# Regrouping the clustering's products and moving the next image's keys, queries and first scores, with the first transfers on two queues

## The chip, the cores and the metric

One core of one Trainium2 chip runs the kernel. The metric is device time in microseconds of one launch, the median of three runs. Everything is fp32.

## What is computed

The input x is four images of 256 channels by 64x64 points (N = 4096). Each image goes through two layers:

```python
# layer 0: attention over the 4096 points
attn = softmax((wq x + bq)^T (wk x + bk))
x = gamma * (wv x + bv) attn^T + x
# layer 1: clustering, then a perceptron
y = x + ls1 * cluster(group_norm1(x))
y = y + ls2 * (w2 gelu(w1 group_norm2(y) + b1) + b2)
z = relu(bn(y * dw_w));  z = relu(bn(pw_w z))
```

`cluster` works per head (4 of 24 channels) and per quarter of the image (2x2 folds). It pools 4 centres, gives each point to its most similar centre, averages the points of each centre (this needs the *count* of points per centre), and sends each centre's mean back to its points, weighted by the similarity, through `proj_w`. The group norms are over all channels and points of an image, so group_norm2 needs every point of y before its first output.

## The kernel before

The program is written out in a fixed order; every engine takes its instructions in that order and waits on semaphores. For each of the four images (loop at L1557) it runs `weighting` (the attention's weighted sums, L582), `cluster` (L693) and `mlp` (L1155). TensorE is kept busy across the seams: the next image's projections are a list of small closures (`parts.projections`, L686), and `fill(n)` issues the next n of them wherever the image at hand would make TensorE wait. The list holds 32 halves of v (L307; two share a PSUM bank and one ScalarE copy), and at place 26 `k_half(0)` (L283, keys), `q_four(0)` (L328, queries of four blocks) and `k_half(1)`. For the last image the list holds a block of the third image's perceptron instead (`late_block`, L1039).

The steps that the change and the prediction touch:

- **Start** (L100 to L115). All first loads are issued by SP, in this order: `wqk_s`, `pv_s` (per-partition parameters), four pieces of `bqk_s` (biases of q and k), the first two of the four x tiles (two DMAs of 512 KB each), `wv_s`, `gbv`, the other x tiles, `pc_s`, and so on. `alone` (L531) then projects keys (`kp`, L291) and queries (`qp`, L333), sends the queries to the four row bands through GpSimd's DMA queue, and projects v (`vp`, L314).
- **Count** (L920). After the eight blocks of `fv` (L868), TensorE sums the pooled v (`agg`, L898). VectorE takes norms, the largest similarity and a one-hot (L828 to L834, tile `scr`), which the `cnt` matmuls (L923) wait for. In between stand `similar(1, lambda: fill(2))` and `fill(3)`: the two fills come to five closures.
- **Products back to the points** (`products`, L979; row `op`, L993). There are 16 matmuls with 32 rows each: two halves hb of the points, two halves c of the channels, four quarters q. Quarter q uses rows 32q to 32q+31 of the array, so different quarters can run side by side. For c = 0 they go to `ps_s` banks and VectorE adds them into y (L1005); for c = 1 they go to the `ps_a` banks a0 and a1 (by q % 2), ScalarE scales them (L1017) and GpSimd adds them (L1018). `seen(hb, c)` takes the statistics for group_norm2 on VectorE, four at a time (L977). Five calls of `products` make four unbroken groups on TensorE, with fills between (L1022 to L1035).
- **Second norm** (`group_norm`, L239). VectorE aggregates the statistics (L243), TensorE averages over the partitions (`gnm`, L245 and L246), VectorE takes differences (L249 to L253), TensorE averages again (`gnv`, L255), then come the root on ScalarE and the scale and bias on VectorE. One fill stands after `gnm`, one after `gnv`, then all that is left.
- **Perceptron.** `mlp` first has GpSimd form sums of weights (L1168 to L1173), then norms block 0 (L1187, L1250 to L1253), then runs units (block nb, j) with j from 0 to 3: `hp`, `hq`, `hr` (L1372) and `mo` (L1289). After some units the next image's scores for its first queries are formed (`score`, L352; row `sc`, L363): `at` (L1463) says after which unit. Their copies go to ScalarE; their maxima wait in the list `maxima`, from which `rest` takes one before and one after each unit with j > 1.

Of the kernel before, what the change touches and what calls it, by code (L numbers as in the profile page):

```python
# [8 lines left out]
F32 = mybir.dt.float32  # L9
# [4 lines left out]
P = 128  # L14
# [3 lines left out]
NB = 512  # L18
NBLK = N // NB
XT = 1024  # L20
D = 32
# [24 lines left out]
def attention_then_cluster_block(  # L46
# [37 lines left out]
        nc.sync.dma_start(out=d.rearrange("(a b) -> a b", b=D), in_=rows)  # L84
        nc.sync.dma_start(out=dst, in_=d.partition_broadcast(P))

    def load_x(b, t):
        xb = x[b].rearrange("(k p) h w -> p k (h w)", p=P)
        xt = spool.tile([P, KC, XT], F32, tag="s", name=f"x_{b}_{t}")
        for k in range(KC):  # L90
            nc.sync.dma_start(out=xt[:, k, :], in_=xb[:, k, t * XT : (t + 1) * XT])
        return xt

    def loaded(name, ap, shape):
        t = const.tile(shape, F32, name=name)
        nc.sync.dma_start(out=t, in_=ap)
        return t


    wqk_s = const.tile([P, KC, 2, D], F32, name="wqk_s")  # L100
    for k in range(KC):
        nc.sync.dma_start(out=wqk_s[:, k], in_=wqk[k * P : (k + 1) * P, :, :D])
    pv_s = loaded("pv_s", pv, [P, NPV])
    bqk_s = const.tile([P, 2], F32, name="bqk_s")
    for r in range(RG):
        nc.sync.dma_start(
            out=bqk_s[r * D : (r + 1) * D, :], in_=pv[:D, PV["bq"] : PV["bq"] + 2]
        )
    xs0 = [load_x(0, t) for t in range(2)]
    wv_s = loaded("wv_s", wv.rearrange("(k p) m -> p k m", p=P), [P, KC, C])  # L110
    gbv = const.tile([P, KC], F32, name="gbv")
    nc.sync.dma_start(out=gbv, in_=bv.rearrange("(k p) -> p k", p=P))
    xs0 += [load_x(0, t) for t in range(2, N // XT)]
    pc_s = loaded("pc_s", pc.rearrange("(k p) n -> p k n", p=P), [P, KC, len(PC)])
    h64 = loaded("h64", consts[:, K_H64:K_BD], [P, 64])  # L115

# [52 lines left out]
    def rsqrt(dst, src, eps, meanwhile=lambda: None):  # L169

        nc.vector.tensor_scalar(dst, src, eps, None, ALU.add)
        nc.scalar.activation(dst, dst, AF.Sqrt)
        meanwhile()
        nc.vector.reciprocal(dst, dst)
# [60 lines left out]
    def table(f):  # L235

        nc.scalar.activation(probe, probe, f)

    def group_norm(b, which, stats, fill, meanwhile=lambda: None):  # L239

        nm = f"{which}_{b}"
        mv = small.tile([P, 2], F32, tag="mv", name=f"mv_{nm}")
        nc.vector.bn_aggr(mv, stats.rearrange("p i s -> p (i s)"))  # L243
        ps1 = ps_a.tile([P, NB], F32, tag="a0", name=f"gnm_{nm}")
        nc.tensor.matmul(ps1[:, 0:1], left, mv[:, 0:1], start=True, stop=True)  # L245
        nc.tensor.matmul(ps1[:, 1:2], avg, mv[:, 0:1], start=True, stop=True)  # L246
        fill(1)
        dv = small.tile([P, 2], F32, tag="dv", name=f"dv_{nm}")
        nc.vector.tensor_copy(dv, ps1[:, 0:2])  # L249
        nc.vector.scalar_tensor_tensor(  # L250
            mv[:, 1:2], dv[:, 0:1], dv[:, 0:1], mv[:, 1:2], ALU.mult, ALU.add
        )
        nc.vector.tensor_scalar(dv[:, 1:2], dv[:, 1:2], -1.0, None, ALU.mult)  # L253
        ps2 = ps_a.tile([P, NB], F32, tag="a1", name=f"gnv_{nm}")
        nc.tensor.matmul(ps2[:, 0:1], avg, mv[:, 1:2], start=True, stop=True)  # L255
        rstd = small.tile([P, 1], F32, tag="rstd", name=f"rstd_{nm}")
        rsqrt(rstd, ps2[:, 0:1], GN_EPS, meanwhile)
        fill(3 if which == "gn1" else 1)
        if which == "gn2":
            table(AF.Gelu_apprx_tanh)  # L260
        ga = small.tile([P, KC], F32, tag="ga", name=f"ga_{nm}")
        gb = small.tile([P, KC], F32, tag="gb", name=f"gb_{nm}")
        nc.vector.tensor_scalar(ga, par(f"{which}_w"), rstd, None, ALU.mult)
        nc.vector.scalar_tensor_tensor(gb, ga, dv[:, 1:2], par(f"{which}_b"), ALU.mult, ALU.add)
        return ga, gb
# [9 lines left out]
    def attention(b, xs):  # L275
# [408 lines left out]
        parts.score, parts.fold, parts.q_block = score, fold, q_block  # L684
        parts.maximum, parts.first, parts.exps = maximum, first, exps
        parts.projections = [lambda i=i: v_half(i) for i in range(N // P)]  # L686
        parts.projections[26:26] = [lambda: k_half(0), lambda: q_four(0), lambda: k_half(1)]
        return parts


    h64_q = h64[:ED].rearrange("p (q h m) -> p q h m", q=4, h=HEADS)

    def cluster(b, ys, stats, cells, rest, fill, gelu):  # L693

        pool = small.tile([P, KC, 4, 4], F32, tag="pool", bufs=1, name=f"pool_{b}")

# [107 lines left out]
        def over_m(t):  # L804
            return t.unsqueeze(2).to_broadcast([P, 64, 4])

        def similar(f, meanwhile=lambda: None):

            sg = sgs[f]

            def between():
                table(AF.Gelu_apprx_tanh)
                meanwhile()

            rsqrt(prns[f], prns[f], L2_EPS, between)
            nc.vector.tensor_tensor(quad(sg), quad(sg), over_m(prns[f]), ALU.mult)
            nc.scalar.activation(sg, sg, AF.Tanh, scale=ab[:, 0:1], bias=ab[:, 1:2])
            if f == 0:
                gelu(0)
                table(AF.Sqrt)  # L820
# [85 lines left out]
        fill(2)  # L906
        summed(lambda j, q: pool_w[:, j], True)
        heads(NBLK - 1)
        similar(1, lambda: fill(2))
        gelu(1)  # L910
        fill(3)
        table(AF.Sqrt)
# [63 lines left out]
            for q in range(4):  # L976
                nc.vector.bn_stats(stats2[:, 4 * q + 2 * hb + c, :], pieces[hb, c, q])  # L977

        def products(hb, c, qs):  # L979
            if c == 0:  # L980
                two = [
                    ps_s.tile([P, 2, NB], F32, tag="s", name=f"op_{b}_{hb}_{c}_{f}")
                    for f in range(2)
                ]
                ops = {q: two[q // 2][:, q % 2, :] for q in qs}
            else:
                ops = {
                    q: ps_a.tile([P, NB], F32, tag=f"a{q % 2}", name=f"op_{b}_{hb}_{c}_{q}")
                    for q in qs
                }  # L990
            for q in qs:
                rows = slice(q * 32, (q + 1) * 32)
                nc.tensor.matmul(  # L993
                    ops[q],
                    g_s[rows, c * P : (c + 1) * P],
                    sim_t[rows, hb, :],
                    start=True,
                    stop=True,
                )
            for q in qs:  # L1000
                y = pieces[hb, c, q] = ys[2 * (q // 2) + hb][:, c, :].rearrange(
                    "p (h f w) -> p f h w", h=16, f=2
                )[:, q % 2]
                if c == 0:
                    nc.vector.scalar_tensor_tensor(  # L1005
                        y,
                        ops[q].rearrange("p (h w) -> p h w", h=16),
                        par("ls1", c),
                        y,
                        ALU.mult,  # L1010
                        ALU.add,
                    )
                else:
                    add = work.tile(
                        [P, NB], F32, tag=f"w{(4 * hb + q) % 3}", bufs=1, name=f"cl_{b}_{hb}_{q}"
                    )
                    nc.scalar.activation(add, ops[q], AF.Identity, scale=par("ls1", c))  # L1017
                    nc.gpsimd.tensor_tensor(  # L1018
                        y, add.rearrange("p (h w) -> p h w", h=16), y, ALU.add
                    )  # L1020

        products(0, 0, range(4))  # L1022
        products(0, 1, (0, 1))
        seen(0, 0)
        fill(2)
        products(0, 1, (2, 3))
        fill(2)
        products(1, 0, range(4))
        products(1, 1, (0, 1))
        fill(2)  # L1030
        products(1, 1, (2, 3))
        seen(0, 1)
        seen(1, 0)
        seen(1, 1)
        fill(5)  # L1035
        return stats2


# [113 lines left out]
        nc.gpsimd.tensor_tensor(s2, s1, a11, ALU.subtract)  # L1152
        return s1, s2, w7

    def mlp(b, ys, stats2, fill, nxt, blocks, turned):  # L1155


        W_A, W_CD, W_B, W_D = own_w["q"]
# [101 lines left out]

        for _ in norm(0, nc.vector):
            pass
        if nxt:
            nxt.q_block(0, nc.sync)

        def product(out, w, j, x):
            nc.tensor.matmul(out, w[:, j * P : (j + 1) * P], x, start=True, stop=True)
# [179 lines left out]

        hooks, drips, maxima = [], [], []  # L1450

        def hook():
            while hooks:
# [6 lines left out]
        acc, todo, slots = None, iter(()), (0,) * 4  # L1460
        own = ahead = iter(())

        at = {(u, 3): u for u in range(7)} | {(7, 2): 7}  # L1463
        if blocks < NBLK:
            at |= {(6, 1): 6, (6, 2): 7}
            del at[6, 3]
# [86 lines left out]
    with tc.manual_schedule():  # L1553
        here = attention(0, xs0)
        here.alone()
        late = None
        for b in range(B):  # L1557
            xs1, begun = [], []
            nxt = attention(b + 1, xs1) if b + 1 < B else None

            def ahead():
                if nxt and len(xs1) < N // XT:
                    xs1.append(load_x(b + 1, len(xs1)))
                elif late and not begun:
                    begun.append(begin())

            begin, todo, gelu = late or (None, list(nxt.projections) if nxt else [], lambda i: None)
            fill = filler(todo)
            stats, cells, rest = here.weighting(ahead, fill, (lambda: None) if b else derived)
            turned = turn_w2(b, not nxt)  # L1570
            stats2 = cluster(b, here.xs, stats, cells, rest, fill, gelu)

            late = mlp(b, here.xs, stats2, fill, nxt, NBLK - (b == B - 2), turned)
            here = nxt


# [74 lines left out]
```

## Time and profile before

| | us |
|---|---|
| median of 3 runs | 3362.1 (3361.42 to 3362.94) |
| the profiled execution | 3361.72 |
| its span, first to last instruction | 3359.9 |
| TensorE busy | 3308.0 (98%) |
| VectorE busy | 2225.8 (66%) |
| GpSimd busy | 1930.0 (57%) |
| ScalarE busy | 1683.6 (50%) |
| mean granted TensorE clock | 0.998 |

In the lines below, a line gives start and duration in us, engine, source line, operation, output and inputs with shape and type, and in brackets the idle time of that engine before it and what ended it. PE is TensorE, PEld its weight loads, DVE VectorE, ACT ScalarE, POOL GpSimd, SP the queue that issues most DMAs. An fp32 matmul of the program is two records. The granted clock is a share of full speed.

### The profile page before, as it was taken

The numbers are of one execution on the slowest core, as the hardware profiler recorded it, in microseconds if no ns is written. First come the engines' busy times: TensorE is split into PE (matmuls) and PEld (weight loads), VectorE is DVE, ScalarE is ACT, GpSimd is POOL, SyncE is SP. The second block draws the span as 40 slices with busy tenths as digits, with TensorE's granted clock in tenths as the row PEclk, the third lists the DMA queues.
The fourth block names the chain that finished last, engine by engine and source line by source line (L and its number), as shares of the span: only waits on it lengthen the run. The fifth ranks groups of instructions, "written<-read, shape, count | busy, mean of one in ns | idle before, by whom it ended". The sixth has DMA issues, their size and how long they took to land.

```text
span 3359.9 us, 34780 instructions
## 1 busy us (share of the span) xinstructions
PE 3308.0 (98%) x12322; PEld 1807.2 (54%) x12322; DVE 2225.8 (66%) x3546; ACT 1683.6 (50%) x2253; POOL 1930.0 (57%) x1366
## 2 busy tenths in 40 slices
PE   8999999999999999999999999999999999999999
PEld 4333444788533344578843344457873344346786
DVE  4767764677666766467766676646766766665675
ACT  5555553545555554354555555434555555544444
POOL 2655666366365676646635566554644676673664
PEclk9999999999999999999999999999999999999999
DMA  2000002000000000200000000020000000010000
GB/s 72 13 13 10 14 9 86 4 13 20 25 13 13 13 13 17 76 4 20 15 27 13 10 13 13 22 71 4 20 26 13 13 13 13 10 40 1 13 20 26
DMA packets 43102, 70.99 MB, mean 21 GB/s; under 512 B 9680, under 2 KB 18480, under 8 KB 42928
## 3 DMA queue, kind: packets, MB, share of 16 engines
q1 hardware_dynamic: 38064, 61.94, 5.5%
q10 hardware_dynamic: 4608, 6.30, 0.8%
q8 instruction: 97, 1.59, 0.2%
q14 instruction: 77, 0.63, 0.1%
q0 software_dynamic: 256, 0.52, 0.1%
HBM read 43.46 MB, written 16.89 MB: 18 GB/s over the span
## 4 chain that ended last, share of the span: by engine, by line
PE 94%; DVE 5%; ACT 1%; issue 0%; POOL 0%; DMA 0%; SPq 0%; ACTq 0%; POOLq 0%; DVEq 0%
PE av L477 53%; PE mo L1289 10%; PE sc L363 8%; PE hq L1372 5%; PE hp L1372 3%; PE hr L1372 3%; PE vp L314 2%; PE fv L868 2%; PE mo L1273 1%; PE hq_pw L1372 1%; PE pw L1226 1%; PE hr_pw L1372 1%; PE op L993 1%; PE hp_pw L1372 1%; PE qp L333 0%; PE kp L291 0%
## 5 line engine op out<-in xcount | busy, mean ns | idle before, releaser
L477 PE MATMUL av<-s,v 128*128 128x512 f32 x4096 | 1819.2, 598 | 0.6 <-ACT s L467 0.6
L472 POOL TENSOR_TENSOR acc<-acc,s 128x1024 f32<-128x1024 f32 x448 | 1057.2, 2360 | 539.0 <-ACT s L467 520.2
L477 PEld LDWEIGHTS av<-s,v 128*128 128x128 f32 x4096 | 759.0, 190 | 1044.8 <-issue 1034.8
L467 ACT ACTIVATE s<-s 128x1024 f32<-128x1024 f32 x512 | 540.2, 1057 | 592.0 <-DVE s L464 550.6
L464 DVE TENSOR_TENSOR s<-s,mb 128x1024 f32<-128x1024 f32 x512 | 595.7, 1205 | 18.2 <-ACT mb L448 16.3
L385 DVE TENSOR_TENSOR top<-sc,top 128x1024 f32<-128x1024 f32 x196 | 239.4, 1221 | 374.8 <-PE sc L363 374.7
L1327 ACT ACTIVATE hs<-hs,pv_s 128x256 f32<-128x256 f32 x496 | 232.2, 502 | 340.1 <-DVE hs L1363 340.1
L1289 PE MATMUL mo<-hs,w 128*128 128x256 f32 x1512 | 387.8, 382 | 0.0
L381 ACT COPY s<-sc 128x1024 f32<-128x1024 f32 x224 | 224.8, 1003 | 225.6 <-PE sc L363 225.6
L1289 PEld LDWEIGHTS mo<-hs,w 128*128 128x128 f32 x1512 | 282.0, 190 | 60.1 <-ACT hs L1327 19.8
L363 PE MATMUL sc<-q,k 32*128 32x512 f32 x2048 | 300.0, 640 | 0.4 <-ACT s L386 0.4
L388 DVE TENSOR_TENSOR top<-sc,top 128x1024 f32<-128x1024 f32 x196 | 240.0, 1225 | 72.4 <-ACT s L381 59.3
L386 ACT COPY s<-sc 128x1024 f32<-128x1024 f32 x224 | 227.0, 1013 | 66.4 <-DVE top L383 36.1
L1363 DVE TENSOR_TENSOR hs<-hq,hs 128x256 f32<-128x256 f32 x496 | 198.6, 421 | 75.5 <-PE hq L1372 65.3
L469 POOL TENSOR_TENSOR acc<-s 128x1024 f32<-128x1024 f32 x32 | 75.3, 2353 | 287.5 <-ACT s L467 260.8
L1296 POOL TENSOR_TENSOR hs<-hs 128x256 f32<-128x256 f32 x108 | 82.3, 762 | 194.1 <-ACT hs L1380 91.4
L363 PEld LDWEIGHTS sc<-q,k 32*128 32x128 f32 x2048 | 86.4, 182 | 183.2 <-issue 122.0
L1363 DVE TENSOR_TENSOR hs<-hp,hs 128x256 f32<-128x256 f32 x124 | 52.1, 420 | 142.5 <-ACT hs L1380 142.5
L1372 PE MATMUL hr<-xn,w 128*128 128x256 f32 x496 | 127.5, 379 | 0.5 <-DVE hs L1363 0.5
L314 PE MATMUL vp<-wv_s,x 128*128 128x256 f32 x512 | 123.4, 387 | 0.2 <-ACT v L322 0.2
L314 PEld LDWEIGHTS vp<-wv_s,x 128*128 128x128 f32 x512 | 93.5, 190 | 25.5 <-issue 10.5
L1372 PEld LDWEIGHTS hr<-xn,w 128*128 128x128 f32 x496 | 94.1, 190 | 19.1 <-issue 4.8
(261 smaller groups left out, 3508.2 us busy)
## 6 DMA issues: line engine op xcount, KB each, us to landing
x<-in_x SPq DMA_DIRECT2D x32, 512.0 KB, 6.9
out<-xn SPq DMA_DIRECT2D x62, 256.0 KB, 2.1
w<-in_w SPq DMA_DIRECT2D x8, 1024.0 KB, 10.9
mr<-row_mx SPq DMA_DIRECT2D x28, 256.0 KB, 3.1
rden<-row_rd SPq DMA_DIRECT2D x28, 256.0 KB, 3.2
q<-q ACTq DMA_DIRECT2D x96, 64.0 KB, 2.0
mix<-in_wfv SPq DMA_DIRECT2D x8, 192.0 KB, 8.5
q<-q SPq DMA_DIRECT2D x24, 64.0 KB, 2.0
```

Of the source, the lines that this page charges most:

```text
L314: nc.tensor.matmul(vps[0][:, i % 2, :], xs[i * P // XT][:, k, o : o + P], wv_s[:, k, :], start=(k == 0), stop=(k == KC - 1),)
L363: nc.tensor.matmul(halves[r // 2][:, r % 2, :], k_s[rows, g, :], q_s[rows, :], start=True, stop=True)
L385: nc.vector.tensor_tensor(top, halves[1], top, ALU.max)
L388: nc.vector.tensor_tensor(top, halves[0], top, ALU.max)
L464: nc.vector.tensor_tensor(sh, sh, mxs[nb].unsqueeze(1).to_broadcast([P, 2, NB]), ALU.subtract)
L467: nc.scalar.activation(sh, sh, AF.Exp)
L472: nc.gpsimd.tensor_tensor(acc, acc, s[:, 2 * h : 2 * h + 2], ALU.add)
L477: nc.tensor.matmul(av[c], own["v"][:, RG * g + quarter, c * P : (c + 1) * P], slots[u][:, quarter, :], start=(g == 0 and quarter == 0), st ...
L1289: return nc.tensor.matmul(bank[:, half * HB : (half + 1) * HB], a[:, j], t, start=start, stop=stop)
L1327: nc.scalar.activation(src, src, AF.Gelu_apprx_tanh, bias=pvc("b1", P, j + 4 * (i > 1)))
L1363: nc.vector.tensor_tensor(dst, ps, term, ALU.add)
L1372: nc.tensor.matmul(out, w, x, start=True, stop=True)
```

## The change

It has five parts, and no arithmetic changes.

1. The first two DMAs (tile x_0) go on SP at once. The weights of q and k, tile x_1 and the biases are issued by ScalarE's queue, in this order; `pv_s` is loaded after the last x tile.
2. `k_half(0)` and `q_four(0)` move from place 26 of the list to place 16. In `cluster`, the fill of two no longer stands inside `similar(1)` but behind it, so that the tanh comes first on ScalarE.
3. The 16 products come in three groups, of six, six and four. The last two of (1, 1) go to a pair of `ps_s` banks instead of a0 and a1.
4. At the end of `cluster` stand the first queries' transfers (`q_block(0)`, before at L1264), a fill of four, and `score(0)`, before after unit (0, 3) of the perceptron. Without a next image, a fill of six stands there.
5. `group_norm` for gn2 has a fill of two after `gnm`, before one.

```diff
-    def load_x(b, t):
+    def load_x(b, t, dma=nc.sync):
...
-            nc.sync.dma_start(out=xt[:, k, :], in_=xb[:, k, t * XT : (t + 1) * XT])
+            dma.dma_start(out=xt[:, k, :], in_=xb[:, k, t * XT : (t + 1) * XT])
...
+    xs0 = [load_x(0, 0)]
...
-        nc.sync.dma_start(out=wqk_s[:, k], in_=wqk[k * P : (k + 1) * P, :, :D])
-    pv_s = loaded("pv_s", pv, [P, NPV])
+        nc.scalar.dma_start(out=wqk_s[:, k], in_=wqk[k * P : (k + 1) * P, :, :D])
...
+    xs0.append(load_x(0, 1, nc.scalar))
     for r in range(RG):
-        nc.sync.dma_start(
+        nc.scalar.dma_start(
...
-    xs0 = [load_x(0, t) for t in range(2)]
...
     xs0 += [load_x(0, t) for t in range(2, N // XT)]
+    pv_s = loaded("pv_s", pv, [P, NPV])
...
-        fill(1)
+        fill(1 if which == "gn1" else 2)
...
-        parts.projections[26:26] = [lambda: k_half(0), lambda: q_four(0), lambda: k_half(1)]
+        parts.projections[26:26] = [lambda: k_half(1)]
+        parts.projections[16:16] = [lambda: k_half(0), lambda: q_four(0)]
...
-        similar(1, lambda: fill(2))
+        similar(1)
+        fill(2)
...
+        def pair(hb, c, q):
+            two = ps_s.tile([P, 2, NB], F32, tag="s", name=f"op_{b}_{hb}_{c}_{q}")
+            return [((hb, c, q + i), two[:, i, :]) for i in range(2)]
+
+        def single(hb, c, q):
+            return (hb, c, q), ps_a.tile(
+                [P, NB], F32, tag=f"a{q % 2}", name=f"op_{b}_{hb}_{c}_{q}"
+            )
+
-        products(0, 0, range(4))
-        products(0, 1, (0, 1))
+        products(*pair(0, 0, 0), *pair(0, 0, 2), single(0, 1, 0), single(0, 1, 1))
         seen(0, 0)
         fill(2)
-        products(0, 1, (2, 3))
+        products(single(0, 1, 2), single(0, 1, 3), *pair(1, 0, 0), *pair(1, 0, 2))
         fill(2)
-        products(1, 0, range(4))
-        products(1, 1, (0, 1))
-        fill(2)
-        products(1, 1, (2, 3))
+        products(single(1, 1, 0), single(1, 1, 1), *pair(1, 1, 2))
         seen(0, 1)
         seen(1, 0)
         seen(1, 1)
-        fill(5)
-        return stats2
+        if not nxt:
+            fill(6)
+            return stats2
+
+        nxt.q_block(0, nc.sync)
+        fill(4)
+        copies = []
+        nxt.score(0, copies, maxima)
+        copies.pop()()
+        return stats2
...
-        if nxt:
-            nxt.q_block(0, nc.sync)
...
-        at = {(u, 3): u for u in range(7)} | {(7, 2): 7}
+        at = {(u, 3): u for u in range(1, 7)} | {(7, 2): 7}
```

More of the change, by code (lines that the diff above doesn't have):

```diff
@@ L686, in attention, with cluster @@
         parts.projections = [lambda i=i: v_half(i) for i in range(N // P)]
-        parts.projections[26:26] = [lambda: k_half(0), lambda: q_four(0), lambda: k_half(1)]
+        parts.projections[26:26] = [lambda: k_half(1)]
+        parts.projections[16:16] = [lambda: k_half(0), lambda: q_four(0)]
         return parts
     h64_q = h64[:ED].rearrange("p (q h m) -> p q h m", q=4, h=HEADS)
-    def cluster(b, ys, stats, cells, rest, fill, gelu):
+    def cluster(b, ys, stats, cells, rest, fill, gelu, nxt, maxima):
         pool = small.tile([P, KC, 4, 4], F32, tag="pool", bufs=1, name=f"pool_{b}")
@@ L805, in over_m, with similar @@
             return t.unsqueeze(2).to_broadcast([P, 64, 4])
-        def similar(f, meanwhile=lambda: None):
+        def similar(f):
             sg = sgs[f]
[L811 to L815, printed above, removed]
+            rsqrt(prns[f], prns[f], L2_EPS, lambda: table(AF.Gelu_apprx_tanh))
             nc.vector.tensor_tensor(quad(sg), quad(sg), over_m(prns[f]), ALU.mult)
@@ L977, in seen, with products @@
                 nc.vector.bn_stats(stats2[:, 4 * q + 2 * hb + c, :], pieces[hb, c, q])
[L979 to L991, printed above, removed]
+        def products(*jobs):
+            for (hb, c, q), bank in jobs:
                 rows = slice(q * 32, (q + 1) * 32)
                 nc.tensor.matmul(
-                    ops[q],
+                    bank,
                     g_s[rows, c * P : (c + 1) * P],
@@ L999, in products @@
                 )
-            for q in qs:
+            for (hb, c, q), bank in jobs:
                 y = pieces[hb, c, q] = ys[2 * (q // 2) + hb][:, c, :].rearrange(
@@ L1006, in products @@
                         y,
-                        ops[q].rearrange("p (h w) -> p h w", h=16),
+                        bank.rearrange("p (h w) -> p h w", h=16),
                         par("ls1", c),
@@ L1016, in products @@
                     )
-                    nc.scalar.activation(add, ops[q], AF.Identity, scale=par("ls1", c))
+                    nc.scalar.activation(add, bank, AF.Identity, scale=par("ls1", c))
                     nc.gpsimd.tensor_tensor(
@@ L1153, in turn_w2, with mlp @@
         return s1, s2, w7
-    def mlp(b, ys, stats2, fill, nxt, blocks, turned):
+    def mlp(b, ys, stats2, fill, nxt, blocks, turned, maxima):
         W_A, W_CD, W_B, W_D = own_w["q"]
@@ L1446, in finish @@
             return lambda: relu(1)
-        hooks, drips, maxima = [], [], []
+        hooks, drips = [], []
         def hook():
@@ L1570, in attention_then_cluster_block @@
             turned = turn_w2(b, not nxt)
-            stats2 = cluster(b, here.xs, stats, cells, rest, fill, gelu)
-            late = mlp(b, here.xs, stats2, fill, nxt, NBLK - (b == B - 2), turned)
+            maxima = []
+            stats2 = cluster(b, here.xs, stats, cells, rest, fill, gelu, nxt, maxima)
+            late = mlp(b, here.xs, stats2, fill, nxt, NBLK - (b == B - 2), turned, maxima)
             here = nxt
```

## The prediction

> **What bounds the kernel now.** I read the page first, then who waited for whom on TensorE, then the order of time in the start and in one clustering.
>
> ```profile
> PE 3308.0 (98%) x12322; PEld 1807.2 (54%) x12322; DVE 2225.8 (66%) x3546; ACT 1683.6 (50%) x2253; POOL 1930.0 (57%) x1366
> ```
>
> TensorE is busy 98% of the span, and the change neither adds nor removes a matmul. So the time can only come from TensorE's waits, and from places where its rows lie side by side better. The waits of TensorE (us in total, times, longest):
>
> ```profile
> PE kp L291 <- DMA x<-in_x: 9.7, 3, 8.7
> PE cnt L923 <- DVE scr L834: 5.4, 4, 1.4
> PE hp L1372 <- DVE xn L1251: 3.9, 4, 1.5
> PE gnm_gn L245 <- DVE mv_gn L243: 3.8, 4, 3.2
> PE gnv_gn L255 <- DVE dv_gn L253: 2.9, 7, 0.4
> PE hp L1372 <- DVE xn L1187: 2.4, 3, 0.8
> ```
>
> All six lie in the two places that the change edits: the start, and the clustering with the second norm behind it. The longest gnm wait, 3.2, is that of image 3. Now image 0 in order of time (start us, us, engine, line), VectorE and then TensorE:
>
> ```profile
> 630.03 2.73 DVE L1005 SCALAR_TENSOR_TENSOR x<-op,pc_s,x 128x512 f32<-128x512 f32 x4 [2.79 <-PE op L993]
> 632.67 2.46 DVE L977 BATCH_NORM_STATS2 st<-x 128x6 f32<-128x512 f32 x4
> 636.85 2.73 DVE L1005 SCALAR_TENSOR_TENSOR x<-op,pc_s,x 128x512 f32<-128x512 f32 x4 [1.72 <-PE op L993]
> 639.49 7.21 DVE L977 BATCH_NORM_STATS2 st<-x 128x6 f32<-128x512 f32 x12
> ```
>
> ```profile
> 628.85 1.99 PE L993 MATMUL op<-simt,g 32*128 32x512 f32 x12
> ...
> 635.67 1.99 PE L993 MATMUL op<-simt,g 32*128 32x512 f32 x12
> ...
> 647.65 0.28 PE L245 MATMUL gnm_gn<-mv_gn,left 128*128 128x1 f32 x2
> ...
> 653.17 0.67 PE L1372 MATMUL hp<-xn,w_abcd 128*128 128x256 f32 x2 [0.77 <-DVE xn L1251]
> ...
> 675.27 1.14 PE L363 MATMUL sc<-q,k 32*128 32x512 f32 x8
> ```
>
> VectorE is idle 1.72 us because the second half's products reach TensorE only at 635.67. From 636.85 it runs without a break to the aggregate (646.73, 0.59), and gnm follows at 647.65 with no wait. Then come waits of 0.41 (gnv), 0.81 and 0.77 (hp), which the little filler left there can't cover.
>
> **Start.** SP issues weights, parameters and biases ahead of x:
>
> ```profile
> 0.74 1.35 SPq L102 DMA_DIRECT2D wqk_s<-in_wqk  x2
> 2.14 0.60 SPq L96 DMA_DIRECT2D pv_s<-in_pv  x1
> 2.78 1.82 SPq L106 DMA_DIRECT2D bqk_s<-in_pv  x4
> 4.64 1.85 SPq L91 DMA_DIRECT2D x<-in_x  x4
> ...
> 8.69 2.24 PE L291 MATMUL kp<-x,wqk_s 128*32 128x256 f32 x16 [8.69 <-DMA x<-in_x]
> ...
> 13.03 1.08 PE L291 MATMUL kp<-x,wqk_s 128*32 128x256 f32 x8 [0.23 <-DMA x<-in_x]
> ```
>
> The first chunk of x lands 4.05 us after its issue begins, the fourth at 13.03, so a 512 KB chunk takes (13.03-8.69)/3 = 1.45 us. With x_0 first on SP, the first lands at 0.74+4.05 = 4.8. The fourth has two ends. If ScalarE's queue were served as if alone, everything shifts by 4.64-0.74 = 3.9, to 9.1. If wv (half a chunk) and the first chunk of x_2 are both served ahead of it, it is 9.1+2.2 = 11.3; more can't be ahead, because x_2's second chunk waits for the semaphore of x_1's second. Half-and-half sharing gives 4.8+4x1.45 = 10.6, less some head start for x_1, which is queued while x_0 lands: I take 10.3, a gain of **2.7** (1.7 to 3.9). Here the Trainium skill speaks against the change: "DMA: Bandwidth & Descriptors", section "Issuing engines are not separate DMA queues", has all issuers run on the same 16 engines, so that a second issuer saves only the sequencer's time, usually small beside the transfer. By "usually small" the gain is about 0. The rows say 3.9 us of SP's issue time ahead of x against 1.45 for a chunk, so I count it, but give the second queue no bandwidth of its own. ScalarE issues 8 DMAs before its first table load; the last biases wait for x_1's first chunk, and k's copy then comes near 12, when the keys' products have just ended, with the queries' products (2.7 us) still ahead of the v products that need that bank. Late pv, pc and wpw have users 50 us later; the v weights, early on SP, are there in time. The q transfers on POOL's queue shift along.
>
> **Ahead of the count (images 0 to 2).** kp (639.34-637.59 = 1.75) and qp (1.83) go in, five v halves become three (minus 1.8). That is 1.8 more against the wait of 1.33: the wait closes and the count comes 0.4 late. k's and q's copies (0.69 each) stand behind the tanh on ScalarE; v's banks are free before they are wanted. VectorE's chain to the count does not move, since it ran without a wait from the last fv. Image 3 has no such filler and keeps its wait.
>
> **Products in three groups.** A group of six takes 1.92, of two 1.06 (632.69 to 633.75). In group 2 the row bands come as 2,3,0,1,2,3, two slots like the old six; group 3 has all four bands, one slot. 1.92+1.92+1.06 against 5.96: 1.06 saved on TensorE. More important is when the second half starts: 628.85+0.4, +1.92, two v halves 1.92, so group 2 at 633.1 instead of 635.67+0.4. Its banks: ScalarE frees a0 and a1 by 632.6, VectorE the four others by 633.1, just in time. VectorE is through with the first half at 632.67+2.46+0.4 = 635.5 and goes on at once: 636.85 to 647.32 was 10.47, so the aggregate is done at 646.0 and gnm starts at 646.05, **1.6 earlier**. GpSimd's adds (1.28 each) end near 643.8, before VectorE's last four statistics. TensorE is there earlier: group 3 at 637.0 to 638.0, two v halves, kp, one v half (4.6) and the score (1.07) end at 643.7. So a **new wait of 2.3 us** stands before gnm. Behind gnm lie five v halves instead of two (2.7 more) where waits of 1.99 were: hp's second product comes 1.3 earlier (651.85), not 1.6.
>
> **The score** took 1.07 between 675.27 and 676.34; at its new place it lies in the new wait, so the old place gives back 1.07. Nothing there needs it as cover: image 3 has no score at that point and goes on with no wait by VectorE or ScalarE (6.0 us per unit). Its two copies (1.0 each) on ScalarE are over by 645.8, before the root at about 648.7; its two maxima (0.65 each) fall in unit (0,2), where VectorE was idle 1.86 in one piece. q's four transfers go past nothing on SP. Sum per image: 1.3+1.07 = 2.4, times three **7.2**.
>
> **Image 3.** Group 2 at 3107.2 instead of 3110.19, and VectorE is free at 3109.7: gnm at 3120.2 instead of 3121.98. Behind it VectorE's two-input steps last as long as GpSimd's weight sums beside them (1.30, 1.45, 1.37 where alone 0.22 to 0.55), and those start only 0.75 earlier. Between 0.75 and 3 (if the clock stays up); I take **1.6**.
>
> **The clock.** The longest wait of image 3 was followed by this (columns: stretch, busy of PE, PEld, DVE, ACT, POOL, granted clock, DMA share, GB/s):
>
> ```profile
> 3118.00:3120.00 2.00, 0.78 (x2) 0.00 (x0) 2.00 (x5) 0.69 (x1) 1.72 (x2) 1.00 0.00 0
> 3120.00:3122.00 2.00, 0.02 (x1) 0.05 (x1) 1.80 (x4) 1.39 (x2) 0.50 (x2) 0.93 0.00 0
> 3122.00:3124.00 2.00, 2.00 (x6) 1.48 (x7) 0.44 (x3) 0.81 (x1) 1.07 (x2) 0.50 0.00 0
> ```
>
> Half speed, for about 6.6 us. The skill's "TensorE: Matmul & The Clock Gate", Part 1, wants a whole free-running idle window of about 3.4 us for that; here 3.21 was enough. Waits of 1.55 and 1.33 left the clock at 1.00. By the rule 2.3 us costs nothing; by the row, at worst, 3.3 us per image. I take nothing, as 2.3 leaves a third of any such window busy.
>
> **Sum:** 2.7+7.2+1.6 = 11.5. The profiled execution took 3361.7 (span 3359.9 and 1.8 around it): 3350.2. The median of the runs is 0.4 above it: **3350.6**.
>
> **Rivals.** (1) *VectorE's chain does not start earlier*: a bank of group 2 comes back late, or GpSimd's weight sums, now over the norm, hold VectorE as in image 3. For it: the banks are free with almost no margin, and one step at 648.38 lasted 1.09 beside GpSimd. Against: the statistics ran 0.6 each beside GpSimd's adds. Then only the score and the start are left: 2.7+3x(1.07-0.4), about 4.7: 3357.4. Chance 0.12. (2) *The start gives nothing*, since x_1 is fed as slowly as before: 3353.3, 0.10. (3) *The clock drops in the new wait*, two windows as in image 3: 3.3 lost three times, about 3360.5, 0.06. (4) *Slower*: the same drop, but the thin start of the perceptron (TensorE busy 60% from 650 to 654) keeps it down a third window, 10 us: 5 lost per image, 3365.6. It decides from a loss of 11.5/3 = 3.8 per image, 7.7 us at half clock. 0.03. The forecast has 0.69, with 3347 to 3354 as its own range.
>
> A measurement tells 0.2%, 6.7 us, from no change. Below 3355.4: the forecast, (2) and a little of (1), 0.81; within: the rest of (1), (3) and most of (4), 0.17; slower 0.02. The range 3345 to 3358 takes in the ends of the start, of image 3 and (1).
>
> **What would show it.** In the new profile: the second kp of the start waiting for x until 9 to 11; no wait before the count in images 0 to 2; VectorE's second four-step group following its statistics without idle; a wait of about 2.3 before gnm and none before gnv; clock 1.00 there; no score between units (0,3) and (1,0). I am wrong if gnm still comes some 24.4 us after the count, or the clock falls there.

## The result, and the profile after it

The changed kernel takes **3352.97 us** in the median of nine runs (3350.55 to 3355.8), the kernel before 3362.12 beside it (3361.42 to 3364.27): a ratio of 0.9971, interval 0.9961 to 0.9982, or 9.15 us. The forecast was 3350.6. The profiled execution took 3351.63 with a span of 3349.9, so 10.1 less span than before (3349.85 against 3359.94, with one more digit). One execution of a kernel below (keys and queries back) took 3827.59 at a mean granted clock of 0.849; the ratios and the range given there leave it out. Line numbers from here on are those of the changed kernel (products L983, the scaled addition L995, statistics L976, aggregate L245, gnm L247 and L248, gnv L257, the score L365, hp L1373, GpSimd's weight sums L1171 to L1176).

What TensorE waits for now (us in total, times, longest):

```profile
PE gnm_gn L247 <- DVE mv_gn L245: 6.4, 6, 1.9
PE kp L293 <- DMA wqk_s<-in_wqk: 6.0, 1, 6.0
...
PE hp L1373 <- DVE xn L1254: 2.6, 1, 2.6
PE gnm_gn L247 <- ACT xl L1101: 2.6, 1, 2.6
...
PE cnt L922 <- DVE scr L832: 1.4, 1, 1.4
PE kp L293 <- DMA x<-in_x: 1.3, 2, 0.8
```

The first wait of the start is shorter (6.0 instead of 8.7) and is one for the weights of keys and queries, no longer for x. The count waits only in image 3. The wait before gnm has moved into images 0 to 2: 1.92 each, which is most of the 6.4. Image 3 has 2.6 before gnm and 2.6 before hp's second product. (The list puts the first of these down to ScalarE's `xl`, which ended at 3111.08; VectorE's aggregate ended at 3111.07, so the list can't tell the two apart.)

Image 0 in order of time, TensorE and VectorE:

```profile
628.04 2.73 DVE L995 SCALAR_TENSOR_TENSOR x<-op,pc_s,x 128x512 f32<-128x512 f32 x4 [2.79 <-PE op L983]
630.68 2.46 DVE L976 BATCH_NORM_STATS2 st<-x 128x6 f32<-128x512 f32 x4
...
633.06 2.71 DVE L995 SCALAR_TENSOR_TENSOR x<-op,pc_s,x 128x512 f32<-128x512 f32 x4
635.69 7.20 DVE L976 BATCH_NORM_STATS2 st<-x 128x6 f32<-128x512 f32 x12
640.51 1.14 PE L365 MATMUL sc<-q,k 32*128 32x512 f32 x8
643.57 0.38 PE L247 MATMUL gnm_gn<-mv_gn,left 128*128 128x1 f32 x2 [1.92 <-DVE mv_gn L245]
...
649.38 0.67 PE L1373 MATMUL hp<-xn,w_abcd 128*128 128x256 f32 x2
```

The second group is done before VectorE asks for it: the line at 633.06 has no idle time in brackets, where 1.72 stood before. The score is over by 641.65, and TensorE then stands 1.92 until the aggregate. hp's second product, at 649.38, no longer waits.

To place the gain I take two landmarks per image: the first den product of the attention before the clustering, and hp's second product behind the norm. Start to the first den, before and then after:

```profile
574.08 0.43 PE L649 MATMUL den<-rden,ones 128*32 128x128 f32 x8
...
571.96 0.43 PE L651 MATMUL den<-rden,ones 128*32 128x128 f32 x8
```

So 2.1 from the start. From den to hp's second product, and how many windows of half clock (stretches of 3.41 us, explained below) lie between the two:

| kernel | image 0 | image 1 | image 2 | image 3 | windows at half clock |
|---|---|---|---|---|---|
| before | 79.09 | 79.10 | 79.11 | 82.80 | 0, 0, 0, 2 |
| after | 77.42 | 78.83 | 77.44 | 81.70 | 0, 1, 0, 1 |

From there to the next image's den, over the score's old place, 753.50 became 752.53 behind image 0. So image 0 gains 1.67+0.97 = 2.6; den to den, image 1 gains 1.6, image 2 2.7; image 3 gains 1.1. With the start that is 10.1, the whole span's change.

Images 0 to 2 are the same program with the same wait of 1.92, yet image 1 took 1.4 longer. The clock is what differs (columns: stretch, its length, busy of PE, PEld, DVE, ACT, POOL, granted clock, DMA share, GB/s):

```profile
642.21:645.62 3.41, 2.05 (x11) 1.88 (x12) 2.40 (x6) 1.86 (x3) 3.33 (x4) 1.00 0.00 0
1471.65:1475.06 3.41, 1.52 (x9) 1.42 (x10) 2.64 (x6) 1.93 (x2) 3.33 (x3) 1.00 0.00 0
1475.06:1478.47 3.41, 3.41 (x11) 2.79 (x10) 1.39 (x7) 0.79 (x2) 1.44 (x2) 0.50 0.02 5
2301.09:2304.50 3.41, 1.65 (x11) 0.49 (x9) 3.38 (x6) 1.97 (x3) 3.33 (x4) 1.00 0.00 0
```

In image 1 the wait fell almost whole into one stretch (second line, TensorE busy 1.52), and the next ran at half speed. In image 0 the border at 642.21 cut the wait in two and the clock stayed. In image 2 (fourth line) one stretch holds most of the wait and TensorE is busy 1.65, and the clock stayed too; the last section comes back to this.

### The profile page after: what moved, and what is told of

Same layout as the page of the kernel before. It is cut to its first block, busy times and chain, and to the rows that moved or that the text cites. A ratio compares the mean times of both kernels' runs of the same rounds, so it can differ in the third digit from the quotient of the medians.

```text
span 3349.9 us, 34778 instructions
## 1 busy us (share of the span) xinstructions
PE 3302.7 (99%) x12322; PEld 1807.3 (54%) x12322; DVE 2225.7 (66%) x3546; ACT 1683.3 (50%) x2253; POOL 1930.9 (58%) x1366
## 4 chain that ended last, share of the span: by engine, by line
PE 94%; DVE 4%; POOL 1%; ACT 1%; issue 0%; DMA 0%; ACTq 0%; POOLq 0%; DVEq 0%
PE av L479 54%; PE mo L1290 9%; PE sc L365 8%; PE hq L1373 5%; PE hp L1373 3%; PE hr L1373 3%; PE fv L866 3%; PE vp L316 2%; PE mo L1274 1%; DVE st L976 1%; PE hq_pw L1373 1%; PE pw L1229 1%; PE hr_pw L1373 1%; PE hp_pw L1373 1%; DVE x L995 0%; PE qp L335 0%
## 5 line engine op out<-in xcount | busy, mean ns | idle before, releaser
L365 PE MATMUL sc<-q,k 32*128 32x512 f32 x2048 | 299.9, 640 | 0.4 <-ACT s L388 0.4
L365 PEld LDWEIGHTS sc<-q,k 32*128 32x128 f32 x2048 | 86.4, 182 | 183.1 <-issue 122.0
L1373 PE MATMUL hr<-xn,w 128*128 128x256 f32 x496 | 127.5, 379 | 0.5 <-DVE hs L1364 0.5
L1373 PEld LDWEIGHTS hr<-xn,w 128*128 128x128 f32 x496 | 94.1, 190 | 19.1 <-issue 4.8
```

What stands on the lines that cost most here:

```text
L365: nc.tensor.matmul(halves[r // 2][:, r % 2, :], k_s[rows, g, :], q_s[rows, :], start=True, stop=True)
L1373: nc.tensor.matmul(out, w, x, start=True, stop=True)
```

## The experiments

Each kernel's own profile gives the same landmarks; the table with all of them stands behind the last experiment. The diffs are cut to what matters, and `...` marks a gap. The first starts from the kernel before, the others from the changed kernel; what neither diff nor text names is as there.

**The start alone.** The kernel before, with only the start's part of the change (the biases and `pv_s` move too, as there).

```diff
+    xs0 = [load_x(0, 0)]
...
-        nc.sync.dma_start(out=wqk_s[:, k], ...)
+        nc.scalar.dma_start(out=wqk_s[:, k], ...)
...
+    xs0.append(load_x(0, 1, nc.scalar))
...
```

> The kernel before with only the new order of the first transfers. My theory: the start is worth what the first v product gains in the traces (16.55 to 14.54), so about 2.1 us, 3360.0, and all images keep their lengths (fv to hp's second product 61.8 us in image 0). Rival, that a second issuing queue saves nothing that the span sees: 3362.1. If the start were worth the 2.7 of the prediction: 3359.4.

Measured: 3360.8 (3359.8 to 3362.04) against 3362.58, ratio 0.9995 (0.9987 to 1.0003). The time alone can't tell that from nothing; the profile can: the first den at 572.04 instead of 574.08, so 2.0, and the four clusterings as before to within 0.02. So the start can be added to the rest. The 2.0 is one draw: in the nine profiles with the new start the first den comes at 571.82 to 572.79, which is 1.3 to 2.3 ahead of the one profile before.

**Keys and queries back behind the count**, the score staying at clustering's end.

```diff
-        parts.projections[26:26] = [lambda: k_half(1)]
-        parts.projections[16:16] = [lambda: k_half(0), lambda: q_four(0)]
+        parts.projections[26:26] = [lambda: k_half(0), lambda: q_four(0), lambda: k_half(1)]
...
+        fill(2)
         nxt.q_block(0, nc.sync)
-        fill(4)
+        fill(2)
```

> The changed kernel with keys and queries back at place 26 of the list (the queries' transfers then stand behind them, before the last two fills). My theory: VectorE's chain from the last fv to hp's second product binds, so the moved filler only shifts where TensorE waits: a wait of about 1.3 before the count comes back, the wait before gnm falls from 1.9 to some 0.3 to 1, and gnm comes no later, about 0.2 earlier (the count is 0.2 earlier). Time within 1 us of the changed kernel's 3353. Rival, that covering the count's wait was itself a gain: three times 1.3 lost, 3357.

Measured: 3362.12, ratio 0.9997 (0.9988 to 1.0006): nearly all the gain is gone, which no theory had. In image 0:

```profile
640.80 2.45 SPq L350 DMA_DIRECT2D q<-q  x4
...
642.92 2.93 PE L365 MATMUL sc<-q,k 32*128 32x512 f32 x8
...
643.64 0.59 DVE L245 BATCH_NORM_AGGREGATE mv_gn<-st 128x2 f32<-128x96 f32 x1
...
645.78 0.38 PE L247 MATMUL gnm_gn<-mv_gn,left 128*128 128x1 f32 x2
```

VectorE has its aggregate at 644.23, but TensorE is inside the score, which lasts 2.93 instead of 1.14 because each of its row bands waits for its transfer of the queries, issued only from 640.80 on. gnm stands behind it in order and comes 1.5 late. The wait sits inside the group of the score, so the list of waits shows only 1.3 of it, in image 2. In images 1 and 2 the clock dropped on top. The runs, 3355.59 to 3367.54, go with the mean granted clock (0.998 in the fastest, 0.995 in the slowest), so much of the loss is the clock's.

**The filler spread around gnm.** Six closures ahead of the score instead of four, and one instead of two directly behind gnm in images 0 to 2.

```diff
-        fill(1 if which == "gn1" else 2)
+        fill(1 if which == "gn1" or b < B - 1 else 2)
...
         nxt.q_block(0, nc.sync)
-        fill(4)
+        fill(6)
```

> The changed kernel with the same filler dealt out anew in images 0 to 2: six closures before the score instead of four, one behind gnm instead of two. My theory: the wait before gnm shrinks from 1.92 to under 0.5, gnv no longer stands behind filler and comes about 0.4 earlier, so 0.4 per image, and the clock does not drop in images 0 to 2. Image 3 may still drop. Profile about 1.3 shorter at equal drops; median about 3350.5, and the runs lie closer together. Rival, that the drops have nothing to do with the new wait: they come as often, and the median is not below 3352.

Measured: 3350.42 (3349.2 to 3350.74), ratio 0.9962 (0.9950 to 0.9975). As expected: gnm at the same place (643.75), the wait before it 0.20, and no half clock in images 0 to 2.

```profile
643.75 0.38 PE L247 MATMUL gnm_gn<-mv_gn,left 128*128 128x1 f32 x2 [0.20 <-DVE mv_gn L245]
```

**Four groups again** (6, 2, 6 and 2 products), with keys, queries and score as in the change. The third fill of two between the groups is taken from the one behind them, so that the filler ahead of gnm is the same.

```diff
-        products(single(0, 1, 2), single(0, 1, 3), *pair(1, 0, 0), *pair(1, 0, 2))
-        fill(2)
-        products(single(1, 1, 0), single(1, 1, 1), *pair(1, 1, 2))
+        products(single(0, 1, 2), single(0, 1, 3))
+        fill(2)
+        products(*pair(1, 0, 0), *pair(1, 0, 2), single(1, 1, 0), single(1, 1, 1))
+        fill(2)
+        products(single(1, 1, 2), single(1, 1, 3))
...
-            fill(6)
+            fill(4)
...
-        fill(4)
+        fill(2)
```

> The changed kernel with the products again in four groups (6, 2, 6, 2) and the same number of fills before the score. My theory: what counts is when the second half's products reach VectorE. They come 3.0 later than with three groups, VectorE idles about 1.7 again, gnm comes about 1.8 later per image, and the wait before gnm is longer (2.5 to 3), so the clock may drop more. Five to nine us lost, 3358 to 3362. Rival, that grouping only saves TensorE's slot: 1.06 per image, which lies in the wait before gnm, so nothing lost, 3353.

Measured: 3363.98, ratio 1.0003 (0.9995 to 1.0011). VectorE's idle 1.72 is back, and with it the work taken from behind gnm:

```profile
635.25 2.73 DVE L995 SCALAR_TENSOR_TENSOR x<-op,pc_s,x 128x512 f32<-128x512 f32 x4 [1.72 <-PE op L983]
637.89 7.21 DVE L976 BATCH_NORM_STATS2 st<-x 128x6 f32<-128x512 f32 x12
645.13 0.59 DVE L245 BATCH_NORM_AGGREGATE mv_gn<-st 128x2 f32<-128x96 f32 x1
```

gnm comes 1.9 later with respect to den in images 0 to 2 and 1.8 in image 3, TensorE waits 12.3 before it in all (longest 3.2), and the clock drops in each. Early score and keys without the three groups are a loss of 3.2 against the start alone (3360.8), the halved clock included.

**The score back in unit (0,3)**, keys and queries staying ahead of the count.

```diff
-        copies = []
-        nxt.score(0, copies, maxima)
-        copies.pop()()
...
-        at = {(u, 3): u for u in range(1, 7)} | {(7, 2): 7}
+        at = {(u, 3): u for u in range(7)} | {(7, 2): 7}
```

> The changed kernel with the first score again in unit (0,3) of the perceptron; keys and queries stay ahead of the count. Theory (the score fills the wait before gnm and its old place gives its length back): the wait before gnm in images 0 to 2 grows from 1.9 to 3.0, the old place takes 1.0 again and loses the wait of 0.2 behind it, so 0.8 per image, 2.4 in all, and the longer wait drops the clock more often, 1.1 each time: 3356.5, between 3355 and 3359. Rival (the score's new place is worth nothing, because it only moves work from one busy stretch to another): 3353 as with the whole change.

**Groups only.** The same, and keys, queries and the queries' transfers at their old places too.

```diff
-        parts.projections[26:26] = [lambda: k_half(1)]
-        parts.projections[16:16] = [lambda: k_half(0), lambda: q_four(0)]
+        parts.projections[26:26] = [lambda: k_half(0), lambda: q_four(0), lambda: k_half(1)]
...
-        nxt.q_block(0, nc.sync)
...
+        if nxt:
+            nxt.q_block(0, nc.sync)
```

> The changed kernel with the score again in unit (0,3), and keys and queries again behind the count, with the transfers of the queries issued behind the first norm: of the change only the three groups, the fillers beside the norm and the start are left. Theory (keys ahead of the count matter because the score at clustering's end needs its queries; covering the count's wait is worth little by itself, since VectorE's chain behind it is fixed): within 1.5 us of the kernel with only the score back, about 3357.5. Rival (the count's wait is what counts; filling it is worth its 1.3 us per image): 3 to 4 us above the kernel with only the score back, 3360 or more.

Measured on one chip: score back 3358.64, ratio 0.9988 (0.9981 to 0.9994); groups only 3356.12, ratio 0.9981 (0.9973 to 0.9989). The first is as expected: the wait before gnm is 2.99 instead of 1.92, the old place takes its 0.9 again, and the clock is halved in every image. The second misses both theories: keys ahead of the count, without the score, cost 2.5 us instead of gaining something. TensorE waits about the same either way: in one piece of 2.99 before gnm (first line, score back), or in two, 1.33 before the count and 1.40 before gnm (groups only):

```profile
643.97 0.38 PE L247 MATMUL gnm_gn<-mv_gn,left 128*128 128x1 f32 x2 [2.99 <-DVE mv_gn L245]
...
621.76 1.57 PE L921 MATMUL cnt<-scr,ones 128*96 128x64 f32 x16 [1.33 <-DVE scr L831]
...
644.11 0.38 PE L247 MATMUL gnm_gn<-mv_gn,left 128*128 128x1 f32 x2 [1.40 <-DVE mv_gn L245]
```

What differs is the clock: 1, 0 and 1 half windows in images 0 to 2 with the two short waits, 1, 1 and 2 with the long one. That is one profile of each; over all runs the mean granted clock was 0.997 or 0.998 with the short waits and 0.996 or 0.997 with the long one. Filling the count's wait alone moves it to gnm; in these runs it paid only with a score there to fill it again.

**Weight sums of image 3.** First the changed kernel without three of GpSimd's four sums (w_bcd and w3_s like w_bac below), then the kernel with the spread filler, in which image 3 has two of the sums on VectorE behind the norm (and not on GpSimd; this part is not in the second diff).

```diff
-        nc.gpsimd.tensor_tensor(w_bac, w_abcd, W_D, ALU.add)
+        if nxt:
+            nc.gpsimd.tensor_tensor(w_bac, w_abcd, W_D, ALU.add)
+        else:
+            nc.gpsimd.memset(w_bac, 0.0)
```

> The changed kernel with three of GpSimd's four weight sums of image 3 (w_bac, w_bcd, w3) replaced by zeros, so the last image's output is not the reference's. Theory (these sums hold VectorE's norm in image 3): the steps of the norm take 0.4 to 0.7 each, hp's second product of image 3 comes 2.6 us earlier with respect to gnm, the wait of 2.6 before it is gone, and the time is 3350.4. Rival (VectorE's steps are long for another reason): the wait stays at 2 us or more, and the time at 3353.

```diff
         for _ in norm(0, nc.vector):
             pass
+        if not nxt:
+            nc.vector.tensor_tensor(w_bcd, W_B, w_abcd, ALU.subtract)
+            nc.vector.tensor_tensor(w3_s, s2_s, a12_s, ALU.add)
```

> The kernel with the filler spread around gnm, and in image 3 two of GpSimd's four weight sums (w_bcd and w3) moved to VectorE behind the first block's norm. Theory (in image 3 GpSimd's two-input steps hold VectorE's norm): the norm's steps behind w_bac take 0.4 to 0.7 instead of 1.4 to 1.5, hp's second product comes 1.9 us earlier, and the two sums cost VectorE 1.4 behind it, of which half is waited for: 3349.0, between 3348.3 and 3349.6. Rival (the norm waits for something else, or VectorE's later steps eat what is gained): 3350.4 as without the move, or more.

Measured: without the sums 3351.21, ratio 0.9969 (0.9957 to 0.9980); sums moved **3349.14** (3348.11 to 3349.57), ratio 0.9961 (0.9949 to 0.9974), the fastest here. In the second, GpSimd makes its two remaining sums in image 3 from 3114.53 to 3117.13; VectorE beside and behind them:

```profile
3114.63 1.18 DVE L266 SCALAR_TENSOR_TENSOR gb_gn<-ga_gn,dv_gn,pc_s 128x2 f32<-128x2 f32 x1
3115.85 1.57 DVE L1192 TENSOR_SCALAR xn<-x,ga_gn,gb_gn 128x512 f32<-128x512 f32 x1
3117.45 0.43 DVE L1255 TENSOR_TENSOR xn<-xn 128x256 f32<-128x256 f32 x1
3117.80 0.54 DVE L1192 TENSOR_SCALAR xn<-x,ga_gn,gb_gn 128x512 f32<-128x512 f32 x1
```

While GpSimd sums, VectorE's steps take 1.18 and 1.57; from 3117.45 on, with GpSimd idle, 0.43 and 0.54. In the changed kernel the last two took 1.37 and 1.48. So it is not only the two-input steps, as the prediction had it: L1192 takes one 128x512 tensor and two columns. hp's second product comes 1.9 earlier with respect to gnm in both kernels (8.4 instead of 10.2). Without the sums I had expected 2.6, but w_abcd stays, with a VectorE step of 1.18 beside it, and the zeros are written from 3117.85 to 3119.30, with a step of 1.62 beside them. Of the 1.9, the moved kernel shows 1.3 in its time (3349.14 against 3350.42, measured on another chip). In its profiled run a second window at half clock, ahead of image 3, takes 1.5 away again. The spread kernel's profile has one behind hp's second product of image 3 instead (3119.53), so each has three in all.

All landmarks, den to hp's second product. Windows at half clock outside this stretch are not counted: every kernel, the one before too, has one or two at the end of image 2's perceptron, and the groups-only and spread kernels have one right behind hp's second product of image 3.

| kernel | image 0 | image 1 | image 2 | image 3 | windows at half clock |
|---|---|---|---|---|---|
| start alone | 79.10 | 79.11 | 79.12 | 82.79 | 0, 0, 0, 2 |
| keys back | 78.81 | 80.16 | 83.59 | 81.69 | 0, 1, 2, 2 |
| score back | 78.83 | 78.84 | 80.09 | 81.70 | 1, 1, 2, 2 |
| groups only | 78.68 | 77.32 | 78.99 | 81.68 | 1, 0, 1, 1 |
| four groups | 80.71 | 81.01 | 82.39 | 82.79 | 1, 1, 2, 2 |
| filler spread | 77.04 | 77.09 | 77.08 | 81.69 | 0, 0, 0, 1 |
| no sums | 77.44 | 78.84 | 79.12 | 79.81 | 0, 1, 1, 2 |
| sums moved | 77.07 | 77.11 | 77.09 | 79.81 | 0, 0, 0, 1 |

## Why the prediction was right, step by step

**The start: 2.7 forecast, 2.1 came.** x_1's second chunk is used at 10.43 (10.3 forecast). The queries' products before (first line), and the start after:

```profile
13.88 2.74 PE L333 MATMUL qp<-x,wqk_s 128*32 128x512 f32 x16
...
0.75 1.40 ACTq L104 DMA_DIRECT2D wqk_s<-in_wqk  x2
...
6.03 1.97 PE L293 MATMUL kp<-x,wqk_s 128*32 128x256 f32 x16 [6.03 <-DMA wqk_s<-in_wqk]
...
10.43 1.08 PE L293 MATMUL kp<-x,wqk_s 128*32 128x256 f32 x8 [0.55 <-DMA x<-in_x]
11.29 3.32 PE L335 MATMUL qp<-x,wqk_s 128*32 128x512 f32 x16
```

Two things differ. The first keys wait until 6.03 for their weights, issued at 0.75 beside x_0, instead of until 4.8 for x; that costs nothing, as the last chunk decides. And the queries' products last 3.32 instead of 2.74, which is the missing 0.6. No wait stands there; it is the clock. Their records start in sets of four, 0.85 us apart at first and 0.43 later, and the pace changes where the profile's record of the granted clock begins, with 1.00: at 15.59 before, at 14.16 after. If the time ahead of that point counts half, the products take 1.8 in both kernels. The spread kernel's profile bears this out: there the record begins at 9.98, and the products last 1.90:

```profile
10.91 1.90 PE L335 MATMUL qp<-x,wqk_s 128*32 128x512 f32 x16
14.17 1.99 PE L316 MATMUL vp<-wv_s,x 128*128 128x256 f32 x8 [1.37 <-ACT k L300]
```

So x came 2.6 earlier but full speed only 1.4 earlier, a term that the forecast did not have. Its second row shows a further limit close behind: k's copy, forecast near 12, ends at 14.12 there (14.07 in the changed kernel), because the biases land only at 12.1 and a table load of 1.28 comes first, and v waits for it.

The Trainium skill's "DMA: Bandwidth & Descriptors", section "Issuing engines are not separate DMA queues", by whose "usually small" the gain was about nothing, was rightly set aside in its size: the start alone shows 2.0. That all issuers share the same 16 DMA engines, the other half of the section, fits: between 4 and 6 us these were busy 0.18 of the time before and 0.97 after, so what was gained is an earlier start of the transfers. No run issues the new order on one queue, so how much is the order and how much the second queue is not shown.

**Count, groups, score: 2.4 per image forecast, 2.6 where the clock holds.** gnm came 2.0 earlier by den (73.57 to 71.61), with 1.6 forecast; the wait before it is 1.92, not 2.3; hp's second product 1.67 against 1.3; the score's old place gave 0.97, not 1.07. The count came 0.2 later by den, not 0.4. The forecast's own terms behind gnm (1.6 earlier, 2.7 more of filler, 1.99 of waits gone) come to 0.9 and not to its 1.3; the filler took 4.49 instead of 2.22, so 2.27 more and not 2.7. "Nothing there needs it as cover" was not quite so: behind it a product (hp at 672.18) now waits 0.21 for GpSimd's part of the norm. The mechanism is borne out by the four groups, which bring back VectorE's idle time and 1.9 of gnm's. But the parts aren't separate sums: score and keys lose 3.2 without the groups, the start and the groups without them leave 6.4 of the 9 us, and either one back alone leaves 3.9 (score) or 0.5 (keys).

**Image 3: 1.6 forecast, 1.1 came.** gnm comes 1.78 earlier by den, as worked out. Of this 0.7 is lost in VectorE's norm beside GpSimd's sums, the limit that was named; moving two of the sums gives 1.9.

**The clock: the term that was mis-sized.** "I take nothing, as 2.3 leaves a third of any such window busy": a third busy is not enough (the last section has the counts). The wait of 1.92 halved the clock in one image of three, for one window, which cost 1.4 up to hp's second product and 1.1 by the next den. In the profiled run (3351.63, forecast 3350.2) the terms are 0.6 of the start, 0.5 of image 3 and this 1.1, less 0.7 won in images 0 to 2. The median is 1.3 above that run, about what one window more costs. Both bounds that I had weighed were off. The rule of the Trainium skill's "TensorE: Matmul & The Clock Gate", Part 1, a whole idle window, gives no drop, yet none of the drops behind the norms of images 0 to 2, in any kernel, followed a window without work (the emptiest had 0.58 us, in the four-groups kernel). The row of image 3 gave two windows (6.83 us by the clock's record, not 6.6), or 3.3 us of loss; one window came. Rival 3 had the mechanism right and its price too high; rival 4's third window came in no norm. Rivals 1 and 2 fall: VectorE's chain is earlier and so is the start. By the prediction's own sign of being wrong, "or the clock falls there", it was wrong in one image of three. That the sum came so near is in part luck: what images 0 to 2 won above the forecast (0.7) covered more than half of that drop, and whether a wait of 1.92 halves the clock was decided in each image anew. In the runs of the changed kernel the time goes with the mean granted clock: 3350.55 at 0.998, 3352.97 at 0.997, 3355.8 at 0.996.

## What to carry to other kernels

Moving work out of a late stretch paid here only once the work behind it could run earlier: VectorE's second half had to start earlier first, and then the early score, its queries already in place, filled the hole that this opened. A closed wait is to be followed to the next one in order: filling the count's wait only moved it to gnm. Where a wait wasn't filled, two short ones took 2.5 us less than one long one, and two closures moved from behind the wait to ahead of it, in each of three images, were worth about as much (3350.42 against 3352.97).

## What was not expected of the hardware

The granted clock works on a fixed grid. In all ten profiles every stretch at half clock lasted 3.41 or 6.83 us, and in one profile their starts lie whole multiples of 3.413 apart: in the changed kernel 1475.06, 2519.54 and 3113.46, which are 306 and 174 windows. From one profile to the next the grid lies differently against the program. Laid over all ten profiles, from the first record of the clock to 3340 us, it gives this count of full-speed windows, and of those that half speed followed:

| TensorE busy in the window | windows | followed by half speed |
|---|---|---|
| up to 1.41 us | 23 | 23 |
| 1.47 to 1.86 | 12 | 7 |
| 1.87 to 2.12 | 54 | 4 |
| more | 9593 | 1 |

In the last one the score of the keys-back kernel waited inside its group for the queries. So what counts is not the length of a wait but how much of one window it empties. In the middle, TensorE's busy time doesn't decide alone: with 1.52 busy the clock dropped in image 1 of the changed kernel, with 1.65 it stayed in image 2, and of the three windows with a wait of 1.40 in the groups-only kernel two, with 2.02 and 2.01 busy, were followed by half speed and the third, with 2.01, was not. The busy time counts two of gnm's products of one column at 0.38, which may be why; that was not tested.
